# Last three blocks of an attention and FFN kernel: where the normalisation runs, how late squares are added, and the order of the last five steps

## The chip, the core and the metric

The kernel runs on one core of one Trainium2 chip. The metric is the device time in microseconds (us) of one execution. The core has five engines with instruction streams of their own, which meet only through semaphores: TensorE (PE, matmuls; PEld is its weight load), VectorE (DVE), ScalarE (ACT), GpSimd (POOL) and SyncE (SP, which here only issues DMAs). Each engine works its queue in order, so an instruction that waits holds up everything written behind it on the same engine.

## The reference, cut to what matters

The input is 8 sequences of 1024 tokens with 256 channels, in float32. It passes through an attention layer, a layernorm, an FFN and a last layernorm:

```python
x = _layernorm(x + attn(x))          # linear attention, 16 heads, state per sequence
x = _layernorm(x + ffn(x))           # what follows is ffn
h = layer_norm(x, ln1_g, ln1_b)
h = h @ ternary_quant(w1).T + b1     # 256 -> 1024
h = gelu(h)
h = layer_norm(h, ln2_g, ln2_b)      # over the 1024 hidden units
out = h @ ternary_quant(w2).T + b2   # 1024 -> 256
```

The second `layer_norm` needs, for each token, the sum and the sum of squares of 1024 hidden values. The kernel takes the norm out of the product: it multiplies the plain gelu values with w2 and corrects by mean and variance afterwards. The last `_layernorm` is, for each token, `x * rs + sh`, with `rs` the inverse root of the variance and `sh = -mean * rs`. That multiply-add is the "normalisation" of this change.

## The kernel before, in words

The tokens are cut into 16 blocks of 512 (`blocks`, numbered 0 to 15); each block is four tiles of 128 tokens by 256 channels. The program walks through steps; in step i several blocks are in work at once, at different stages: the attention of a block first, then its FFN, then its normalisation. Steps 16 to 20 only drain what is left. What every engine does, and in which order, is written out by hand: the lists in `ORDER` (line 901) hold one word for each piece of work, and `piece` (line 945) issues it. The lists "16" to "20" belong to the last five steps. The words that matter here:

- `H` issues one chunk of the hidden layer (`hidden`, line 653): a block has 8 chunks of 128 hidden units. On TensorE four matmuls (L661) fill one PSUM bank; then ScalarE does the gelu (L667), the upper half of a split of the value into two parts (L670, "u0") and the square (L651). VectorE adds the lower half (L688, "u1", in `lower`; for every third chunk of blocks 13 and 14 it does u0 as well, L687). Below, H14.3 is chunk 3 of block 14, and gelu 14.3, sq 14.3, u0 14.3, u1 14.3 are its steps. u1 is what gives the PSUM bank back. There are two banks named `ph` for H and one named `tp`.
- `A` and `B` issue the second product for one chunk (L733), for tiles 0 and 1 (`A`) and tiles 2 and 3 (`B`), four matmuls each. After chunk 7 ScalarE copies the result out (L746, `z`).
- `ti` transposes the FFN's input of a block (L633); ScalarE writes one part of it (L637, "hThi"), VectorE the other (L638, "hTlo"). All four parts of a block must stand before its first H can end.
- The squares of a block are summed in the tile `sums`: the first two chunks are written there directly, chunks 2 to 5 are added by DMAs that GpSimd issues (L696, two of them), and for blocks 13 and 14 the pair of chunks 6 and 7 is added by one GpSimd instruction over 128x1024 (L694). `sh` then adds the tile's two halves (L712), `sq` transposes the sums on TensorE (L718, "psq") and VectorE reduces them (L720, "sn"). For block 15 GpSimd adds the halves and chunk 6 (two L712), and `sr` adds chunk 7 on VectorE.
- `m` takes steps from queues of small VectorE work (`more`). One such sequence, `rest` (line 794), follows each block's `sq`: statistics of the hidden layer, a power on GpSimd (L143), the two big additions into x per tile (L805, L810), and the statistics of x (`bn_stats` L814, `bn_aggr` L816). Its `rs` is then used in the `rest` of the next block.
- `finish` (line 841) is the normalisation: VectorE makes `sh` (L844), GpSimd does four multiply-adds of 128x256 (L847, "fin"), SyncE sends the block out (L850). It is called for block i-1 in the middle of `rest` of block i, and for block 14 at the end of its own. Block 15 is done apart, by halves (L828 to L839).
- `p` issues one multiply-add of the first layernorm on ScalarE (L894), and `en` four GpSimd instructions that need them (L616).

Three PSUM banks named `w` are handed round: in the last blocks the two B results, the bank of psq and two `ti` take the next one each, and a taker waits until the last user's data are read.

Of the kernel before, what the change touches and what calls it, by code (L numbers as in the profile page):

```python
# [11 lines left out]
AF = mybir.ActivationFunctionType  # L12
ALU = mybir.AluOpType
# [12 lines left out]
def attn_ffn_postln_kernel(  # L26
# [11 lines left out]
    nc = tc.nc  # L38
    B, N, C = x.shape
    HID = w1.shape[1]  # L40
    D = 16
    H = C // D
# [24 lines left out]
    blocks = [(b, g) for b in range(B) for g in range(NB)]  # L67
    xs = {}

    def of_block(dram, i):  # L70
        b, g = blocks[i]
        return dram[b].rearrange("(p t) c -> p t c", p=P)[:, g * G : (g + 1) * G, :]

    def load(i):
        if i < len(blocks):
            xs[i] = xpool.tile([P, G, C], F32, tag="x", name=f"x_{i}")
            nc.sync.dma_start(xs[i], of_block(x, i))
# [247 lines left out]
    def x_of(i):  # L325
        return xs[i]
# [279 lines left out]
    h0, hT, ph, u, sq, sqs, sums, sn, pf, mv, rs, sc, ms, zs = ({} for _ in range(14))  # L606
# [76 lines left out]
    def lower(n):  # L683

        i, j = n // HC, n % HC
        if upper_on_vector(n):
            nc.vector.tensor_scalar(u[n][:, 0, :], ph[n], gm[:, j : j + 1], None, ALU.mult)  # L687
        nc.vector.scalar_tensor_tensor(  # L688
            u[n][:, 1, :], ph[n], gm[:, j : j + 1], u[n][:, 0, :].bitcast(F32),
            ALU.mult, ALU.subtract,  # L690
        )
        if j % 2 == 1 and 1 < j < (HC if i < len(blocks) - 1 else HC - 2):
            if i > len(blocks) - 4 and j == HC - 1:
                nc.gpsimd.tensor_tensor(sums[i], sums[i], sq[i], ALU.add)  # L694
            else:
                nc.gpsimd.dma_start(sums[i], sq[i], accum_op=ALU.add)  # L696

    def upper_on_vector(n):

        return len(blocks) - 4 < n // HC < len(blocks) - 1 and n % 3 == 1  # L700
# [93 lines left out]
    def rest(i, tiles):  # L794
# [3 lines left out]
        if 0 < i < len(blocks) - 1:  # L798
            finish(i - 1, rs[i - 1])
# [24 lines left out]
        if i < len(blocks) - 1:  # L824
            finish(i, r)
            return
# [14 lines left out]
    def finish(i, rs):  # L841

        sh = small.tile([P, G], F32, tag="sh", name=f"sh_{i}")
        nc.vector.scalar_tensor_tensor(sh, mv[i][:, :, 0], -1.0, rs, ALU.mult, ALU.mult)  # L844
        for t in range(G):
            x_t = x_of(i)[:, t, :]
            nc.gpsimd.tensor_scalar(  # L847
                x_t, x_t, rs[:, t : t + 1], sh[:, t : t + 1], ALU.mult, ALU.add
            )
        nc.sync.dma_start(of_block(out, i), x_of(i))  # L850
        load(i + XBUFS)

# [36 lines left out]
    def apply(n):  # L889

        for _ in range(n):
# [19 lines left out]
            m1 m3 ti0/ph B m2 m3 B m m2 p p B sh  # L911
        """,
        "16": """
            p H m1 m2 m6 p H st0/tp m3 A H sq/w m H m st1/tp A H A m8 H A st2/tp st3/w m1 H A m2
            A H tq0/w m1 p m3 a/tp m4 A a/w A a/w m3 tq1/pf a/ph p m2 a/w a/w B B p m4 en m1 m2 p
            m4 a/tp m B sh B B B m m1 ti0/ph m2 m ti1/ph a/tp m p m1
        """,
        "17": """
            m4 m4 B B H m3 m4 m1 H sq/w en m2 B p A m8 H m4 H p A B m4 H m4 ti1/ph en p p m3 A H
            A H A p p p p m4 H A B B A p B  # L920
        """,
        "18": """
            m4 m6 B m3 sh ti0/ph m1 B A B p H H m4 H m2 p p m1 p H ti1/w A ti0/w sq/w m1 m1 m4 H
            H m1 A B m6 B m1 m3 p H B p H p m1 H A B m2 H A B H sh m1 H m4 m4 B H
        """,
        "19": """
            A B p A p A A p B sq/w m4 m4 H A A H m4 m4 B m1 H B m6 A m8 A sh m4 B A B sr B m4 m2
            m3 A B B sq/w B m4 A
        """,
        "20": """  # L930
            m4 m4 B m4 A m4 p
        """,
    }

# [10 lines left out]
    def piece(what, i):  # L945
# [4 lines left out]
        if what == "H":  # L950
            one = turn("H", CHUNKS)
            if one:
                assert count["ti"] >= (one[0] // HC + 1) * KC
                hidden(one[0])
                if low:
                    lower(low.pop())
                low.append(one[0])
        elif low:
            lower(low.pop())
# [150 lines left out]
```

## Time and profile before

| | us |
|---|---|
| median of 3 runs | 666.11 (665.57 to 666.84) |
| the profiled execution | 667.08 |
| its span in the profile | 665.4 |
| PE busy in the span | 605.4 (91%) |
| DVE busy | 511.3 (77%) |
| ACT busy | 498.3 (75%) |
| POOL busy | 338.6 (51%) |
| mean granted TensorE clock | 0.974 |

The span runs from the first to the last profiled instruction; 1.68 us of the profiled execution lie around it. The busy shares are means over a long steady part, in which PE is nearly always at work, and a drain of some 90 us in which it is not: PE is busy for 0.90 to 1.00 of the stretches from 480 to 570 us, and from 570 to 661 us it stands still in places. The change lies in that drain. Times below are us from the start of the span.

### The profile page before, as it was taken

What the parts mean: (1) busy time and instruction counts of PE and PEld (TensorE: products, weight loads), DVE (VectorE), ACT (ScalarE), POOL (GpSimd) and SP (SyncE); (2) the same over time, 40 slices, a digit from 0 to 9 for tenths busy, and PEclk for the clock granted to TensorE, in tenths of its full rate; (3) what the DMA queues carried; (4) which work ended last, traced back from release to release, by engine and by line L of the source; (5) the groups of instructions that cost most, each with busy time, mean ns of one, the idle gap of its engine ahead of it and who ended that gap; (6) DMA issues with size and microseconds to landing.
All of it is one profiled execution on the core that took longest, in us unless ns stands there. A gap on an engine that the chain in (4) does not pass through costs nothing.

```text
span 665.4 us, 9546 instructions
## 1 busy us (share of the span) xinstructions
PE 605.4 (91%) x3200; PEld 478.2 (72%) x3200; DVE 511.3 (77%) x1448; ACT 498.3 (75%) x939; POOL 338.6 (51%) x315
## 2 busy tenths in 40 slices
PE   5799989999999999999999999999999989778850
PEld 3467657878787787868787887878787777566750
DVE  1666776388877797888978887888878888867886
ACT  2554388798897979787887979797979887758720
POOL 1123453545464645646455646456464644765461
PEclk9999999999999999999999999999999999978875
DMA  8522232545365563637463755635354644372321
GB/s 289 208 33 33 32 49 47 96 80 96 48 159 80 115 122 83 129 67 151 80 149 59 159 79 119 120 82 103 61 121 75 125 75 107 56 119 70 89 63 64
DMA packets 33889, 64.73 MB, mean 97 GB/s; under 512 B 3344, under 2 KB 21776, under 8 KB 33840
## 3 DMA queue, kind: packets, MB, share of 16 engines
q0 software_dynamic: 25328, 43.92, 39.8%
q1 hardware_dynamic: 8240, 19.94, 7.9%
q8 instruction: 25, 0.41, 0.3%
q10 hardware_dynamic: 272, 0.26, 0.1%
q14 instruction: 24, 0.20, 0.1%
HBM read 11.95 MB, written 8.39 MB: 31 GB/s over the span
## 4 chain that ended last, share of the span: by engine, by line
PE 64%; DVE 12%; ACT 10%; DMA 4%; issue 4%; POOL 4%; SPq 1%; POOLq 0%; DVEq 0%
PE ph L661 13%; PE pf L733 11%; PE po L546 9%; PE pk L362 8%; PE pa L451 7%; PE pq L408 6%; DVE u L688 3%; ACT sq L651 2%; ACT ph L667 2%; DMA sums<-sums 2%; PE pth L633 2%; PE ptq L341 1%; PE pte L395 1%; PE ptx L341 1%; DVE x L805 1%
## 5 line engine op out<-in xcount | busy, mean ns | idle before, releaser
L733 PE MATMUL pf<-t,u 128*128 128x258 f32 x1024 | 164.0, 300 | 2.3 <-DVE u L688 1.3
L661 PE MATMUL ph<-hT,t 128*128 128x512 f32 x512 | 149.7, 423 | 13.3 <-DVE u L688 10.0
L733 PEld LDWEIGHTS pf<-t,u 128*128 128x128 f32 x1024 | 141.7, 194 | 14.9 <-DVE u L688 4.1
L688 DVE SCALAR_TENSOR_TENSOR u<-ph,gm,u 128x512 fp32r<-128x512 f32 x128 | 95.3, 748 | 51.8 <-ACT sq L651 47.2
L661 PEld LDWEIGHTS ph<-hT,t 128*128 128x128 f32 x512 | 92.0, 192 | 41.0 <-DVE u L688 16.7
L667 ACT ACTIVATE ph<-ph,bh 128x512 f32<-128x512 f32 x128 | 85.1, 665 | 24.1 <-PE ph L661 23.3
L546 PE MATMUL po<-sm,qT 128*128 128x384 f32 x256 | 93.0, 488 | 0.0
L670 ACT ACTIVATE u<-ph,gm 128x512 fp32r<-128x512 f32 x123 | 84.7, 689 | 4.0
L696 POOL DMA_DIRECT2D sums<-sq x45 | 41.5, 923 | 58.3 <-DMA sums<-sq 17.4
L616 POOL TENSOR_SCALAR h<-x,rs_all 128x256 f32<-128x256 f32 x64 | 64.6, 1208 | 7.2 <-ACT x L894 6.2
L651 ACT ACTIVATE sq<-ph,shift 128x512 f32<-128x512 f32 x96 | 65.4, 682 | 0.1
L143 POOL TENSOR_TENSOR ny_y<-nvy,mhalf 128x8 f32<-128x8 f32 x16 | 27.1, 1696 | 74.7 <-DVE nvy L585 74.7
L435 POOL TENSOR_TENSOR q<-q,rq 128x1024 f32<-128x1024 f32 x16 | 31.4, 1962 | 61.2 <-DVE rq L434 59.1
L451 PE MATMUL pa<-x,ek 128*128 128x256 f32 x256 | 60.6, 380 | 0.2 <-ACT ek L399 0.2
L408 PE MATMUL pq<-wqkv_sb,xT 128*128 128x256 f32 x256 | 58.8, 382 | 0.0
L362 PE MATMUL pk<-xT,wqkv_sb 128*128 128x512 f32 x128 | 58.0, 593 | 0.4 <-DVE q L412 0.4
L546 PEld LDWEIGHTS po<-sm,qT 128*128 128x128 f32 x256 | 43.8, 190 | 20.2 <-ACT sm L533 3.0
L422 POOL TENSOR_TENSOR q<-q,qm 128x1024 f32<-128x1024 f32 x16 | 30.9, 1933 | 52.2 <-DVE qm L421 50.1
L451 PEld LDWEIGHTS pa<-x,ek 128*128 128x128 f32 x256 | 47.4, 190 | 9.5 <-ACT ek L399 0.9
L408 PEld LDWEIGHTS pq<-wqkv_sb,xT 128*128 128x128 f32 x256 | 48.5, 191 | 8.0 <-issue 1.2
L637 ACT ACTIVATE hT<-pth,gs 128x512 fp32r<-128x512 f32 x32 | 21.9, 688 | 33.3 <-PE pth L633 33.3
L143 POOL TENSOR_TENSOR ny_f<-nv_f,mhalf 128x8 f32<-128x8 f32 (+2 forms) x17 | 26.6, 1563 | 30.5 <-DVE nv_f L780 30.4
(171 smaller groups left out, 1149.1 us busy)
## 6 DMA issues: line engine op xcount, KB each, us to landing
sums<-sq POOLq DMA_DIRECT2D x45, 512.0 KB, 4.6
x<-in_x_dram SPq DMA_DIRECT2D x16, 512.0 KB, 6.6
x<-crow POOLq DMA_DIRECT2D x16, 512.0 KB, 5.5
x<-bout POOLq DMA_DIRECT2D x16, 512.0 KB, 5.5
out_dram<-x SPq DMA_DIRECT2D x15, 512.0 KB, 2.7
sums<-sums POOLq DMA_DIRECT2D x13, 256.0 KB, 6.1
w<-in_w_dram SPq DMA_DIRECT2D x4, 512.0 KB, 8.0
wqkv_sb<-in_wqkv_dram SPq DMA_DIRECT2D x2, 256.0 KB, 6.7
```

Of the source, the lines that this page charges most:

```text
L143: nc.gpsimd.tensor_tensor(y, v, mhalf[:, :n], ALU.pow)
L362: nc.tensor.matmul(pk, wqkv_sb[:, k, C + c * P : C + (c + 1) * P], xT[i][:, k, :], start=(k == 0), stop=(k == KC - 1),)
L408: nc.tensor.matmul(pq[:, n, :], xT[i][:, k, (t + n) * P : (t + n + 1) * P], wqkv_sb[:, k, 0:C], start=(k == 0), stop=(k == KC - 1),)
L451: nc.tensor.matmul(pa[i][:, c, :], ek[i][:, t, c * P : (c + 1) * P], x_of(i)[:, t, :], start=(t == 0), stop=(t == G - 1),)
L546: nc.tensor.matmul(po[:, c * P : c * P + P + C], qT[i][:, c, t * P : (t + 1) * P], sm[b][:, c, :], start=(c == 0), stop=(c == KC - 1), ski ...
L616: nc.gpsimd.tensor_scalar(h0[i][:, t, :], x_of(i)[:, t, :], rs2[:, t : t + 1], None, ALU.mult)
L651: nc.scalar.activation(sqs[n], ph[n], AF.Square, bias=shift)
L661: nc.tensor.matmul(ph[n], t1[:, k, j * P : (j + 1) * P], hT[i][s][:, k, :], start=(s == 0 and k == 0), stop=(s == 1 and k == KC - 1),)
L667: nc.scalar.activation(ph[n], ph[n], AF.Gelu, bias=bh[:, j : j + 1])
L670: nc.scalar.activation(u[n][:, 0, :], ph[n], AF.Copy, scale=gm[:, j : j + 1])
L688: nc.vector.scalar_tensor_tensor(u[n][:, 1, :], ph[n], gm[:, j : j + 1], u[n][:, 0, :].bitcast(F32), ALU.mult, ALU.subtract,)
L733: nc.tensor.matmul(pf[i, m][t], u[n][:, s, (2 * m + t) * P : (2 * m + t + 1) * P], t2[:, j, :], start=(j == 0 and s == 0), stop=(j == HC - ...
```

## The change

Three things change, all in the last blocks.

1. `finish` for blocks 13 and 14 uses four ScalarE activations (Identity, with bias and scale) in place of four GpSimd `tensor_scalar`. Blocks 0 to 12 keep GpSimd.
2. The addition of chunks 6 and 7 into `sums` for blocks 13 and 14 becomes two GpSimd instructions over 128x512 each.
3. The lists "16" to "20" are replaced.

```diff
             if i > len(blocks) - 4 and j == HC - 1:
-                nc.gpsimd.tensor_tensor(sums[i], sums[i], sq[i], ALU.add)
+                for s in range(2):
+                    half = sums[i][:, s, :]
+                    nc.gpsimd.tensor_tensor(half, half, sq[i][:, s, :], ALU.add)
...
         for t in range(G):
-            x_t = x_of(i)[:, t, :]
-            nc.gpsimd.tensor_scalar(
-                x_t, x_t, rs[:, t : t + 1], sh[:, t : t + 1], ALU.mult, ALU.add
-            )
+            x_t, sh_t, rs_t = x_of(i)[:, t, :], sh[:, t : t + 1], rs[:, t : t + 1]
+            if i < len(blocks) - 3:
+                nc.gpsimd.tensor_scalar(x_t, x_t, rs_t, sh_t, ALU.mult, ALU.add)
+            else:
+                nc.scalar.activation(x_t, x_t, AF.Identity, bias=sh_t, scale=rs_t)
...
         "17": """
-            m4 m4 B B H m3 m4 m1 H sq/w en m2 B p A m8 H m4 H p A B m4 H m4 ti1/ph en p p m3 A H
-            A H A p p p p m4 H A B B A p B
+            p m4 B H m3 m4 m1 H m4 sq/w en m2 m4 B p A m8 H H p B A m4 H m4 ti1/ph en p m3 A H A
+            H A p p p p m4 H A B B A p sh B
         """,
         "18": """
-            m4 m6 B m3 sh ti0/ph m1 B A B p H H m4 H m2 p p m1 p H ti1/w A ti0/w sq/w m1 m1 m4 H
-            H m1 A B m6 B m1 m3 p H B p H p m1 H A B m2 H A B H sh m1 H m4 m4 B H
+            m4 p m6 B m3 ti0/ph m4 m4 B m1 A p B H H H m2 p p m1 p H ti1/w A m1 sq/w m1 m1 m1 m4
+            H H A p m1 B m6 B ti0/w m1 m3 p H H p H m1 A B m2 H A B H m3 H sh B m2 B m1 B H m2 A
         """,
         "19": """
-            A B p A p A A p B sq/w m4 m4 H A A H m4 m4 B m1 H B m6 A m8 A sh m4 B A B sr B m4 m2
-            m3 A B B sq/w B m4 A
+            A A p p A p B sq/w m8 H A m2 A H p B m1 p B m6 m8 A m2 sh H m4 B sr A B B A m2 B m3 B
+            B A sq/ph B A
         """,
         "20": """
-            m4 m4 B m4 A m4 p
+            m4 m4 m4 m3 m2 p A
         """,
```

(List "16" changes in the same way; its words shift by a place or two.) Read out word by word, the new lists give these orders on the engines, beside the old ones:

- TensorE: the second `ti` of block 15 goes from before H14.4 to after B14.1, just ahead of H14.6. psq 13 goes ahead of H14.4 by one place with it. B14.2 to B14.4 go behind one H each, and B14.6 goes from the run of six products behind H15.4 to the place ahead of H15.4. H15.7 goes behind B15.1 and A15.2. At the end B15.7 and A15.5 come ahead of psq 15, and only A15.6 and A15.7 follow it. psq 15 takes a `ph` bank. In the round of the `w` banks psq 14 now follows B14's first bank.
- ScalarE: hThi 15.1 goes from before gelu 14.4 to between sq 14.5 and gelu 14.6. The four fin of block 13 stand between sq 15.6 and gelu 15.7, those of block 14 behind sq 15.7.
- VectorE: hTlo 15.1 goes from before sn 13 to behind the power of block 13. L810 of tile 0 of block 13 goes ahead of u0 and u1 14.6. L805 of tile 2 of block 13 goes ahead of u1 15.1. u1 15.7 goes from between the first L805 and L810 of block 14 to behind the second `bn_stats` of block 14. `sr` goes ahead of the last `bn_aggr` of block 14 and the statistic that starts its last power. The end of that power and the `sh` of block 14 move from before sn 15 to among the statistics of block 15. The `bn_stats` of tile 2 of block 15 moves behind those of tiles 0 and 1.
- GpSimd: for block 13 the two half additions and the L712 now stand in one row ahead of the fin of block 11 (before: L694, fin of block 11, L712). For block 14 the L712 stands behind the DMA for chunks 2 and 3 of block 15 (before: right behind L694). The fin of blocks 13 and 14 are gone.
- SyncE: the outputs leave in the same order.

More of the change, by code (lines that the diff above doesn't have):

```diff
@@ L913, in attn_ffn_postln_kernel @@
         "16": """
-            p H m1 m2 m6 p H st0/tp m3 A H sq/w m H m st1/tp A H A m8 H A st2/tp st3/w m1 H A m2
-            A H tq0/w m1 p m3 a/tp m4 A a/w A a/w m3 tq1/pf a/ph p m2 a/w a/w B B p m4 en m1 m2 p
-            m4 a/tp m B sh B B B m m1 ti0/ph m2 m ti1/ph a/tp m p m1
+            p H m1 m2 m6 p H st0/tp m3 A m1 H sq/w m H A st1/tp m H A m8 H st2/tp st3/w m3 H A A
+            m2 A H m1 tq0/w p m3 a/tp A a/ph m4 A a/w m3 tq1/pf a/ph m2 a/w a/w B B p en m4 m4 m1
+            m2 p m a/tp B sh B B B m m m1 ti0/ph m2 ti1/ph B a/tp m p m1
         """,
         "17": """
-            m4 m4 B B H m3 m4 m1 H sq/w en m2 B p A m8 H m4 H p A B m4 H m4 ti1/ph en p p m3 A H
-            A H A p p p p m4 H A B B A p B
+            p m4 B H m3 m4 m1 H m4 sq/w en m2 m4 B p A m8 H H p B A m4 H m4 ti1/ph en p m3 A H A
+            H A p p p p m4 H A B B A p sh B
         """,
         "18": """
-            m4 m6 B m3 sh ti0/ph m1 B A B p H H m4 H m2 p p m1 p H ti1/w A ti0/w sq/w m1 m1 m4 H
-            H m1 A B m6 B m1 m3 p H B p H p m1 H A B m2 H A B H sh m1 H m4 m4 B H
+            m4 p m6 B m3 ti0/ph m4 m4 B m1 A p B H H H m2 p p m1 p H ti1/w A m1 sq/w m1 m1 m1 m4
+            H H A p m1 B m6 B ti0/w m1 m3 p H H p H m1 A B m2 H A B H m3 H sh B m2 B m1 B H m2 A
         """,
         "19": """
-            A B p A p A A p B sq/w m4 m4 H A A H m4 m4 B m1 H B m6 A m8 A sh m4 B A B sr B m4 m2
-            m3 A B B sq/w B m4 A
+            A A p p A p B sq/w m8 H A m2 A H p B m1 p B m6 m8 A m2 sh H m4 B sr A B B A m2 B m3 B
+            B A sq/ph B A
         """,
         "20": """
-            m4 m4 B m4 A m4 p
+            m4 m4 m4 m3 m2 p A
         """,
```

## The prediction

> **What bounds the drain now.** I read the busy time by stretches first. It shows where the time can come from:
>
> ```profile
> 595.00:600.00 5.00, 2.79 (x15) 2.03 (x14) 4.93 (x8) 2.05 (x6) 2.71 (x2) 1.00 0.22 42
> 600.00:605.00 5.00, 1.95 (x7) 1.27 (x6) 4.83 (x13) 3.99 (x7) 3.50 (x5) 0.87 0.25 105
> ...
> 625.00:630.00 5.00, 5.00 (x30) 4.82 (x30) 4.44 (x15) 2.51 (x7) 0.00 (x0) 0.74 0.55 105
> 630.00:635.00 5.00, 5.00 (x37) 4.65 (x35) 2.46 (x9) 4.79 (x8) 2.54 (x2) 1.00 0.21 43
> 635.00:640.00 5.00, 3.12 (x27) 2.92 (x25) 4.83 (x13) 0.82 (x2) 4.13 (x5) 1.00 0.38 78
> 640.00:645.00 5.00, 0.00 (x0) 0.00 (x0) 4.79 (x12) 0.00 (x0) 2.22 (x3) 0.63 0.22 93
> ```
>
> The columns are the stretch, its length, busy PE, PEld, DVE, ACT and POOL, the granted TensorE clock and the DMAs. From 595 to 605 and from 635 to 645 VectorE is full (4.8 to 4.9 of 5) and TensorE is not (1.95 and 0.00). So a microsecond of VectorE counts there; TensorE's counts in 625 to 630, where it is full at a clock of 0.74.
>
> Next, the timeline says what VectorE does there (start, duration, engine, line, instruction, count; in brackets the idle time before it and who ended it):
>
> ```profile
> 597.29 2.66 POOL L694 TENSOR_TENSOR sums<-sums,sq 128x1024 f32<-128x1024 f32 x1 [4.91 <-DMA sums<-sq]
> ...
> 598.29 1.94 DVE L810 SCALAR_TENSOR_TENSOR x<-g2sum,ms,x 128x256 f32<-128x256 f32 x1
> ...
> 603.85 2.07 PE L661 MATMUL ph<-hT,t 128*128 128x512 f32 x4 [3.05 <-DVE u L688]
> ...
> 618.32 2.40 POOL L694 TENSOR_TENSOR sums<-sums,sq 128x1024 f32<-128x1024 f32 x1 [0.97 <-DMA sums<-sq]
> ...
> 618.80 2.20 DVE L805 SCALAR_TENSOR_TENSOR x<-z,sc,x 128x256 f32<-128x256 f32 x1
> ...
> 620.80 1.34 POOL L712 TENSOR_TENSOR sums<-sums 128x512 f32<-128x512 f32 x1
> 621.04 1.38 DVE L810 SCALAR_TENSOR_TENSOR x<-g2sum,ms,x 128x256 f32<-128x256 f32 x1
> ...
> 623.13 1.20 PE L661 MATMUL ph<-hT,t 128*128 128x512 f32 x4 [1.82 <-DVE u L688]
> 624.17 4.54 PE L733 MATMUL pf<-t,u 128*128 128x258 f32 x24
> ```
>
> L805 and L810 take 0.48 elsewhere. Here they take 1.38 to 2.20, and each ends 0.28 after the GpSimd addition ends: 600.23 after 599.95, 621.00 after 620.72, 622.42 after 622.14. An addition of two SBUF tiles on VectorE is thus held until GpSimd's is done, then let in before GpSimd's next. What reads PSUM (u1 at 602.29 to 605) or one tile (`bn_stats`, 0.43 during L435 at 495.35) is not held. Two of these holds reach TensorE: u1 14.0 comes late, so H14.3 waits 3.05; u1 15.1 comes late, so H15.4 waits 1.82.
>
> **The halves, block 13.** [...] u0 and u1 14.0 are 1.0 earlier, so H14.3 starts at 602.9: -1.0. GpSimd itself does 4.0 us of additions for 3.9 before, and its next work (DMA at 607.64) has 4.1 us of idle time ahead. The fin of block 11, behind them, ends at 604.0 and only an output waits for it.
>
> **hThi and hTlo 15.1, and L810 13.0.** ScalarE has no idle time from 609.31 to 623.76. hThi (0.70) used to lie ahead of that and now lies in it: the 1.0 shrinks to 0.3 at gelu 14.6. On VectorE hTlo (0.73) now stands behind the power of block 13 and L810 (0.48) ahead of u0 and u1 14.6, whose bank H15.1 waits for: sq 14.5 ends at 611.95, then u1 14.5 0.74, power 0.6, hTlo 0.70, three small 0.5, L805 and L810 0.95, u0 and u1 1.45 give 616.85; before, H15.1 started at 616.81. So all of the 1.0 is given back there: 0.0 at gelu 15.1. If nothing had been gained before, the same row would be 0.6 late.
>
> **The halves, block 14.** Its second DMA is issued behind the power of block 13, some 1.5 earlier (611.9 for 613.56), and lands 4.6 later (613.56 to 618.2 before): halves at 616.7 to 619.3. They hold the first L805 13.1 by some 0.8, where L694 and L712 held two by 1.72 + 0.90. L712 is issued only behind the DMA for block 15, which waits for sq 15.3 (623.7): it meets `bn_stats`. u1 15.1 ends at about 621.2 (before 623.08), though one more L805 stands ahead of it. H15.4 then follows B14.4 to B14.6 without a wait, at 622.6, and ScalarE's 0.61 of idle time before gelu 15.4 goes: -0.6.
>
> **B14.6 out of the run.** Behind H15.4 stand 20 matmuls in place of 24, at 0.19 each (4.54 / 24) or at 0.123 (4.91 / 40, at 633.21, clock 1.00). psq 14 now waits for the copy of B14's first bank (two of the four, 0.3 each, about 0.5 behind the last product). At the slow rate H15.5 comes 0.5 earlier, at the fast 1.7. In the trace the slow stretch follows the wait of 1.82, and the rows without such a wait before them (611 to 616, 631 to 638) run fast; the wait goes, so I take -1.7.
> [...]
>
> **ScalarE's new instructions.** A 128x256 Identity takes 0.594 (L894, median of 64; four in a row 2.07). Fin 13 follows its `sh`; behind it wait gelu, u0 and sq 15.7 (0.66 + 0.69 + 0.68): 4.1 us after `sh`. VectorE has eight additions (3.7) and two `bn_stats` (1.1) before it wants u1 15.7, and holds besides, so this costs nothing; without the holds' cover the margin is 0.7. Fin 14 has ScalarE to itself. GpSimd loses 3.13 + 2.18, which brings little: the two L712 of block 15 must wait for a DMA issued at 632.61 (landed 637.2 at 4.6), 1.8 before they used to start, and still hold two additions.
> [...] Here Identity (574.58 to 576.65) stands between Square and Gelu without a gap, so by the trace nothing is added.
>
> **The last chain.** `sr` goes ahead of a `bn_aggr` and a small one: 644.36 comes -0.35. Then psq 15 and sn 15, and VectorE runs the statistics of both halves with the `bn_stats` of tile 2 (0.55) put where VectorE waits for a power: before, the waits were 0.93 and 0.81. The last power of block 14 ends some 0.4 before VectorE wants it. The last normalisations follow as before: -0.2. The order changes of steps 16 and 17 lie before 580, where VectorE and GpSimd wait for the same rows in both; a bank lost or won there is worth at most the 0.4 that PE waits at 546.42, either way: 0.
>
> **Sum**, against the profiled execution (667.08, span 665.4): -1.0 + 1.0 - 0.6 - 1.1 (the rest of -1.7) + 0 - 0.35 - 0.2 = -2.25, span 663.15. That execution is 0.97 above the median, and I take the difference to be the same: 666.11 - 2.2 = 663.9. With a full clock at H14.3 too (2.07 to 1.09) up to 1.0 more goes: 662.9.
>
> **Rivals.**
> - *The slow stretch stays* (the clock falls by itself): -0.5 - 0.35 - 0.2 = -1.05, 665.1. For it: the clock also fell at 641 to 650 in idle time alone. 13%.
> - *The halves are one hold*: GpSimd starts the second before VectorE gets in, and L810 waits until 600.2 as before. Then hThi and hTlo cost their 0.6 at H15.1, and the tail is left: -0.5, 665.6. For it: 0.08 lies between two GpSimd additions (620.72, 620.80). 12%.
> - *Slower: the row of three holds VectorE throughout.* If L810 at 598.4 is not let in until the third addition ends, 597.72 + 3 x 1.34 + 0.28 = 602.0 in place of 600.23, then H14.3 is 1.8 later and nothing is there to take it up, because ScalarE is full from 609 on: -0.45 + 1.8 = +1.4, 667.5. It decides from a hold past 601.9. Against it: in both rows where two additions follow each other one VectorE instruction got in between. 18%.
>
> **Chances.** 57% for the forecast, own range 662.5 to 664.8. 0.2% (1.33 us) is about what a measurement of this kernel tells from no change: faster 57%, within 25% (the first two rivals), slower 18%. The range goes from 662.3 (clock up everywhere, a little more) to 667.0, which leaves out most of the third rival and little below.
>
> **What would show it.** L810 near 598.3 takes under 1.3 and H14.3 waits about 2; no VectorE addition over 1.5 between 616 and 624; H15.4 without a wait; the run behind it at 0.13 a matmul; no gap around the Identities; psq 15 near 642. An L810 over 3 us, or gelu 15.7 behind the wish for u1 15.7, would prove me wrong.

## The result, and the profile after

| us | before | after |
|---|---|---|
| median of 8 runs each, side by side | 667.34 (665.57 to 668.83) | 663.88 (661.26 to 666.66) |
| ratio | | 0.9942, 95% interval 0.9920 to 0.9964 |
| the profiled execution, its span | 667.08, 665.4 | 664.61, 662.9 |
| psq 12 to the last VectorE instruction | 87.73 | 82.67 |
| of it: psq 12 to psq 13 | 34.24 | 30.75 |
| psq 13 to psq 14 | 20.80 | 20.48 |
| psq 14 to `sh` of block 13 | 7.05 | 7.13 |
| `sh` of block 13 to `sr` | 8.76 | 8.08 |
| `sr` to the end | 16.88 | 16.23 |

The changed kernel is faster, by 0.58% (0.36 to 0.80%), or 3.9 us of 667.34. The profiled execution is 2.5 us shorter, but its drain is 5.06 shorter: it comes to psq 12 at 576.11 where the one of before came there at 573.51. Those 2.60 arise ahead of the drain: the granted clock of this execution was 0.99 from 100 to 200 us and 0.98 from 500 to 570, where that of before had 1.00. Over the profiles of all kernels below psq 12 lies between 572.75 and 578.82, and the steady part ahead of it is the same program in all but the words moved in lists 16 and 17 (their worth is measured below). So in what follows the stretches behind psq 12 are compared, besides the times.

The busy time by stretches of the changed kernel, in the columns of the prediction (stretch, length, PE, PEld, DVE, ACT, POOL, granted TensorE clock, DMAs):

```profile
600.00:605.00 5.00, 3.93 (x10) 2.56 (x10) 4.83 (x13) 3.64 (x6) 4.92 (x6) 0.66 0.00 0
...
625.00:630.00 5.00, 4.02 (x30) 3.58 (x29) 4.54 (x17) 3.42 (x9) 2.24 (x3) 1.00 0.57 108
...
635.00:640.00 5.00, 1.89 (x14) 1.49 (x12) 4.86 (x8) 3.54 (x7) 2.70 (x2) 0.85 0.39 131
```

From 625 to 630 the clock is 1.00 where it was 0.74. VectorE is still full at 600 to 605 and at 635 to 640. The low clock has not gone: it lies at 600 to 605 now (0.66 for 0.87).

The timeline of the changed kernel shows the same places as the prediction's (start, duration, engine, line, instruction, count; idle time before it and who ended it). L696 is the addition of chunks 6 and 7 now, L714 the one of the halves, L735 is the second product, L720 is psq, L807 and L812 are the additions into x, L846 is `sh`, L850 the fin on GpSimd and L852 the fin on ScalarE:

```profile
599.74 2.69 POOL L696 TENSOR_TENSOR sums<-sums,sq 128x512 f32<-128x512 f32 x2 [4.93 <-DMA sums<-sq]
...
600.38 0.91 DVE L812 SCALAR_TENSOR_TENSOR x<-g2sum,ms,x 128x256 f32<-128x256 f32 x1
...
600.52 3.83 PE L661 MATMUL ph<-hT,t 128*128 128x512 f32 x9 [2.52 <-DVE hT L638]
604.90 1.20 PE L661 MATMUL ph<-hT,t 128*128 128x512 f32 x4 [0.55 <-DVE u L688]
...
617.61 1.19 PE L661 MATMUL ph<-hT,t 128*128 128x512 f32 x4 [1.51 <-DVE u L688]
...
618.07 2.73 POOL L696 TENSOR_TENSOR sums<-sums,sq 128x512 f32<-128x512 f32 x2 [0.46 <-DMA sums<-sq]
...
618.79 0.85 DVE L807 SCALAR_TENSOR_TENSOR x<-z,sc,x 128x256 f32<-128x256 f32 x1
619.68 1.41 DVE L812 SCALAR_TENSOR_TENSOR x<-g2sum,ms,x 128x256 f32<-128x256 f32 x1
...
622.89 1.09 PE L661 MATMUL ph<-hT,t 128*128 128x512 f32 x4
623.82 2.54 PE L735 MATMUL pf<-t,u 128*128 128x258 f32 x20
625.68 1.60 POOL L714 TENSOR_TENSOR sums<-sums 128x512 f32<-128x512 f32 x1
627.34 0.66 PE L720 MATMUL psq<-ident,sums 128*128 128x128 f32 x4 [0.98 <-POOL sums L714]
...
636.21 1.37 POOL L714 TENSOR_TENSOR sums<-sums 128x512 f32<-128x512 f32 x1 [3.70 <-DMA sums<-sq]
636.38 1.48 DVE L807 SCALAR_TENSOR_TENSOR x<-z,sc,x 128x256 f32<-128x256 f32 x1
...
637.90 1.37 DVE L812 SCALAR_TENSOR_TENSOR x<-g2sum,ms,x 128x256 f32<-128x256 f32 x1
```

The halves do what was expected of them: the held addition of block 12 takes 0.91 (before 1.94), the two held ones of block 13 take 0.85 and 1.41 (2.20 and 1.38), H15.4 has no wait (1.82), and the products behind it run at 2.54 / 20 = 0.127 each (0.19). H14.3 waits 0.55 in place of 3.05, but of these 2.50 only 1.04 are an earlier start, measured from H14.0; in the other 1.46 the matmuls ahead of it run slower (3.83 for 2.37). Two things are new: 1.51 before H15.1 (0.71) and 0.98 of waiting for GpSimd before psq 14. And two additions of block 14 are still held at 636.38 and 637.90, as long as two were before, there those of the next tile (lines of the timeline of before):

```profile
639.19 1.48 DVE L805 SCALAR_TENSOR_TENSOR x<-z,sc,x 128x256 f32<-128x256 f32 x1
640.71 1.37 DVE L810 SCALAR_TENSOR_TENSOR x<-g2sum,ms,x 128x256 f32<-128x256 f32 x1
```

### The profile page after: what moved, and what is told of

It is laid out like the page before. It is cut to its first block, busy times and chain, and to the rows that moved or that the text cites. A ratio compares the mean times of both kernels' runs of the same rounds, so it can differ in the third digit from the quotient of the medians.

```text
span 662.9 us, 9546 instructions
## 1 busy us (share of the span) xinstructions
PE 608.2 (92%) x3200; PEld 479.4 (72%) x3200; DVE 507.2 (77%) x1448; ACT 501.6 (76%) x947; POOL 333.8 (50%) x309
## 4 chain that ended last, share of the span: by engine, by line
PE 70%; DVE 11%; ACT 10%; issue 4%; POOL 3%; DMA 2%; SPq 0%; POOLq 0%; ACTq 0%
PE ph L661 13%; PE pf L735 13%; PE po L546 11%; PE pq L408 7%; PE pk L362 7%; PE pa L451 7%; DVE u L688 2%; ACT ph L667 2%; ACT sq L651 2%; PE pth L633 2%; PE ptq L341 2%; PE ptx L341 2%; PE pte L395 2%; DMA sums<-sums 1%; DMA x<-in_x_dram 1%
## 5 line engine op out<-in xcount | busy, mean ns | idle before, releaser
L735 PE MATMUL pf<-t,u 128*128 128x258 f32 x1024 | 163.3, 299 | 7.2 <-DVE u L688 4.6
L735 PEld LDWEIGHTS pf<-t,u 128*128 128x128 f32 x1024 | 140.6, 192 | 20.3 <-DVE u L688 7.5
L408 PE MATMUL pq<-wqkv_sb,xT 128*128 128x256 f32 x256 | 61.0, 393 | 0.0
L408 PEld LDWEIGHTS pq<-wqkv_sb,xT 128*128 128x128 f32 x256 | 50.0, 197 | 8.7 <-issue 1.2
L362 PEld LDWEIGHTS pk<-xT,wqkv_sb 128*128 128x128 f32 x128 | 24.0, 190 | 24.5 <-issue 20.6
```

Of the source, the lines that this page charges most:

```text
L362: nc.tensor.matmul(pk, wqkv_sb[:, k, C + c * P : C + (c + 1) * P], xT[i][:, k, :], start=(k == 0), stop=(k == KC - 1),)
L408: nc.tensor.matmul(pq[:, n, :], xT[i][:, k, (t + n) * P : (t + n + 1) * P], wqkv_sb[:, k, 0:C], start=(k == 0), stop=(k == KC - 1),)
L735: nc.tensor.matmul(pf[i, m][t], u[n][:, s, (2 * m + t) * P : (2 * m + t + 1) * P], t2[:, j, :], start=(j == 0 and s == 0), stop=(j == HC - ...
```

## The experiments

All in one table: the stretches of the profile as above (us), and the ratio to the kernel before, run on the same chip, side by side. The chips differ a little (medians of before: 667.99, 667.70, 668.06 and 669.93), so ratios are compared, not times.

| kernel | 12 to 13 | 13 to 14 | 14 to `sh` | `sh` to `sr` | `sr` to end | all | ratio (95%) |
|---|---|---|---|---|---|---|---|
| before | 34.24 | 20.80 | 7.05 | 8.76 | 16.88 | 87.73 | 1 |
| scalar_alone | 33.57 | 22.31 | 7.07 | 10.32 | 16.29 | 89.56 | 1.0018 (0.9994 to 1.0042) |
| halves_alone | 31.32 | 17.93 | 7.86 | 8.87 | 16.88 | 82.86 | 0.9965 (0.9941 to 0.9988) |
| halves_scalar | 33.22 | 18.07 | 7.05 | 11.39 | 16.28 | 86.01 | 0.9996 (0.9974 to 1.0018) |
| halves_block13_only | 31.36 | 21.64 | 7.05 | 8.82 | 16.87 | 85.74 | 1.0001 (0.9975 to 1.0026) |
| order_alone | 31.83 | 20.25 | 7.13 | 6.59 | 17.81 | 83.61 | 0.9965 (0.9941 to 0.9989) |
| scalar_order | 33.21 | 20.94 | 7.11 | 8.08 | 16.23 | 85.57 | 0.9971 (0.9947 to 0.9994) |
| halves_order | 30.75 | 20.45 | 7.12 | 6.59 | 17.83 | 82.74 | 0.9969 (0.9940 to 0.9997) |
| after | 30.75 | 20.48 | 7.13 | 8.08 | 16.23 | 82.67 | 0.9942 (0.9920 to 0.9964) |
| late_lists_only | 30.84 | 20.56 | 7.12 | 8.08 | 16.22 | 82.82 | 0.9962 (0.9936 to 0.9987) |
| fin14_on_scalar | 30.76 | 20.34 | 7.11 | 6.59 | 16.15 | 80.95 | 0.9920 (0.9890 to 0.9949) |
| sums_before_dma | 30.74 | 19.79 | 7.05 | 8.08 | 16.21 | 81.87 | 0.9931 (0.9906 to 0.9956) |
| fin14_and_sums | 30.76 | 19.79 | 7.05 | 6.59 | 16.15 | 80.34 | 0.9919 (0.9891 to 0.9947) |
| tail_lists_only | 31.32 | 19.00 | 7.05 | 6.58 | 16.15 | 80.10 | 0.9946 (0.9917 to 0.9974) |

The table tells how far a stretch can be trusted. Up to `sh` of block 13 before and scalar_alone are the same program, and so are halves_alone and halves_scalar: from psq 12 to psq 14 they differ by 0.8 and 2.0. With the new lists and the halves together, six kernels agree within 0.1 from 12 to 13. The two stretches behind `sh` agree within about 0.1 wherever the program there is the same, with one exception: scalar_alone and halves_scalar, 10.32 and 11.39. Each stretch is read from one execution, and the times bear that out only in the main: after, halves_alone, halves_order and late_lists_only have drains of 82.7 to 82.9, and their ratios lie between 0.9942 and 0.9969.

### One part at a time

**halves_alone** takes only the half additions, the lists and the fin as before:

```diff
-                nc.gpsimd.tensor_tensor(sums[i], sums[i], sq[i], ALU.add)
+                for s in range(2):
+                    half = sums[i][:, s, :]
+                    nc.gpsimd.tensor_tensor(half, half, sq[i][:, s, :], ALU.add)
```

> The kernel before with the half additions alone (old lists, normalisation all on GpSimd). Theory (a VectorE addition of two SBUF tiles is held to the end of the GpSimd addition that is running and is then let in): the L810 that took 1.94 near 598 takes about 0.9 to 1.0, H14.3 waits about 2.0 in place of 3.05, and the time falls by 0.5 to 1.3 us (ratio 0.998 to 0.9993). Rival (two additions in a row act as one hold): L810 stays at 1.9, ratio 1.000. Rival (only the order matters): L810 gets shorter but the time stays within 0.3 us.

Its timeline on TensorE, at H14.0, at H14.3 and from H15.4 on:

```profile
600.32 3.92 PE L661 MATMUL ph<-hT,t 128*128 128x512 f32 x9 [2.52 <-DVE hT L638]
605.06 1.21 PE L661 MATMUL ph<-hT,t 128*128 128x512 f32 x4 [0.83 <-DVE u L688]
...
607.82 2.10 PE L661 MATMUL ph<-hT,t 128*128 128x512 f32 x8
...
621.57 1.11 PE L661 MATMUL ph<-hT,t 128*128 128x512 f32 x4
622.52 3.04 PE L735 MATMUL pf<-t,u 128*128 128x258 f32 x24
```

The held addition took 1.27, so GpSimd's two halves are two holds, not one: that rival falls. The gain is larger than the theory's, and H14.3 waits 0.83, not 2.0. TensorE has the same order as before from H14.3 (605.06) to H14.4 (607.82) and needs 2.76 for it, where before needed 4.25 (603.85 to 608.10, with 0.50 of the clock granted from 603.72 to 607.13): 1.5 come from the faster matmuls alone. That part is not sure to come: halves_scalar, the same program to this place, ran slow here (H14.3 took 2.08 for 1.21) and has 33.22 from 12 to 13. At H15.4 there is no wait, and 24 products take 3.04 instead of 4.54 (in before 0.50 of the clock was granted from 624.20 to 627.61): another 1.5 from faster matmuls.

**scalar_alone** takes only the fin of blocks 13 and 14 on ScalarE:

```diff
-            nc.gpsimd.tensor_scalar(...)
+            if i < len(blocks) - 3:
+                nc.gpsimd.tensor_scalar(x_t, x_t, rs_t, sh_t, ALU.mult, ALU.add)
+            else:
+                nc.scalar.activation(x_t, x_t, AF.Identity, bias=sh_t, scale=rs_t)
```

> The kernel before with the normalisation of blocks 13 and 14 on ScalarE alone. Theory (GpSimd is not what the end waits for; its two last additions start with the DMA's landing, about 1.8 us before they used to, and hold two VectorE additions as before): -0.2 to -0.6 us, ratio 0.999 to 0.9997. Rival (taking the normalisation off GpSimd is the main gain): -2 us or more, ratio under 0.997.

Neither theory: no gain in the time (1.0018, the interval holds 1), and by the stretches a loss. `sh` to `sr` is 1.56 longer and `sr` to the end 0.59 shorter. In the old list u1 15.7 stands behind the first L805 of block 14. It needs sq 15.7, which now stands behind four Identities on ScalarE: VectorE waits 3.59 there.

This run shows something else by chance. Its program up to the `sh` of block 13 is that of before, yet the single addition of block 13 caught another VectorE instruction. Its timeline:

```profile
602.45 3.84 PE L661 MATMUL ph<-hT,t 128*128 128x512 f32 x9 [4.29 <-DVE hT L638]
606.59 1.20 PE L661 MATMUL ph<-hT,t 128*128 128x512 f32 x4 [0.30 <-DVE u L688]
```

The L805 ahead of hTlo 14.1 was held for 2.56, and H14.0 waits 4.29 for that part (2.21 in before, where the L810 behind it was caught and H14.3 paid). One addition over 128x1024 thus costs the old order time in either place (12 to 13 is 34.24 and 33.57; with the halves 31.32 to 31.36, or 33.22 where H14.3 ran slow); which place it was differed between these two executions.

**order_alone** takes only the new lists:

```diff
-            m4 m6 B m3 sh ti0/ph m1 B A B p H H m4 H m2 ...
+            m4 p m6 B m3 ti0/ph m4 m4 B m1 A p B H H H m2 ...
...
-            A B p A p A A p B sq/w m4 m4 H A A H m4 m4 ...
+            A A p p A p B sq/w m8 H A m2 A H p B m1 p ...
```

> The kernel before with the five new lists alone: whole additions over 128x1024, normalisation on GpSimd. Theory (the halves give 1.0 us at H14.3 and the order turns it into more): half of the gain of the whole change is left or less, -1 to -2 us, ratio 0.997 to 0.9985; the L810 near 600 is held until the end of the whole addition. Rival (the order does it all): ratio 0.993 to 0.995, as the whole change.

The lists gain as much by themselves as the halves do, 0.9965, a little more than the theory gave them; the L810 near 598 was held to the end of the whole addition as expected (2.16). Half of the gain (2.2 of 4.1 in the drain) is where the prediction saw next to nothing: `sh` to `sr` falls from 8.76 to 6.59. Its timeline there (L847 is the fin on GpSimd, L712 the first of the two additions for block 15, L844 is `sh`, at 632.66):

```profile
632.93 3.52 POOL L847 TENSOR_SCALAR x<-x,ny_f,sh 128x256 f32<-128x256 f32 x4 [2.23 <-DVE sh L844]
...
636.23 0.50 DVE L810 SCALAR_TENSOR_TENSOR x<-g2sum,ms,x 128x256 f32<-128x256 f32 x1
636.43 1.43 POOL L712 TENSOR_TENSOR sums<-sums 128x512 f32<-128x512 f32 x1
...
643.00 2.16 POOL L847 TENSOR_SCALAR x<-x,ny_last,sh 128x256 f32<-128x256 f32 x4 [1.65 <-DVE dev L773]
645.12 0.69 POOL L143 TENSOR_TENSOR ny_f<-nv_f,mhalf 128x2 f32<-128x2 f32 x1
```

With u1 15.7 moved out of VectorE's row, its eight additions are done at 636.7, when GpSimd, busy with the fin until 636.4, has just begun to add: the additions of 1.4 meet `bn_stats`, which is not held: in fin14_on_scalar two of them took 0.41 and 0.39 beside such an addition (L714, 1.42 at 637.22), in before 0.39 to 0.41 with GpSimd idle (642.00 to 644.00). The other side is in the last two lines: the fin of block 14 now stands ahead of the power that the end needs, and VectorE waits 2.28 for that power (`sr` to end: 17.81 for 16.88).

### Two parts at a time

**halves_scalar**, **halves_order** and **scalar_order** join the edits above by twos; the diffs are those shown.

> Both code edits without the new lists. Theory (each edit adds up, and without the lists H15.4 still waits behind u1 15.1 and the run of 24 matmuls stays): -0.8 to -1.8 us, ratio 0.9973 to 0.9988. Rival (the order does it all): ratio 0.999 or above.

> The changed kernel with the normalisation of blocks 13 and 14 back on GpSimd (halves and new lists stay). Theory (ScalarE's four Identities of block 13 free GpSimd too early: its last two additions then meet L807 and L812 of block 14 and cost 1.5 us between the sh of block 13 and sr; behind sr ScalarE gives 0.6 to 1.6 back): sh to sr takes 6.6 in place of 8.1 us, no addition of block 14 is held over 0.7, sr to the end takes 17.5 to 18 in place of 16.2, and the time is that of the changed kernel within 1 us (ratio to before 0.992 to 0.997). Rival (ScalarE's part is worth what the forecast said, GpSimd's load matters): 1.5 us or more slower than the changed kernel, ratio 0.9965 to 0.999.

> The changed kernel with the whole additions over 128x1024 (ScalarE's normalisation and the new lists stay). Theory (the halves give 1.0 at H14.3, most of which is taken back where hTlo 15.1 and L812 stand ahead of u0 14.6): L810 near 598 takes about 2, H14.3 waits over 1.5, and the time is 0.5 to 1.5 us above the changed kernel (ratio 0.9945 to 0.998). Rival (the halves give what they gave alone with the old lists, 2.3 us by the ratio): ratio 0.998 to 1.000.

halves_scalar disappoints as scalar_alone did, for the same reason; its ratio is that of its rival, though the order is not all, as halves_alone shows. On VectorE, in its timeline:

```profile
639.94 0.75 DVE L688 SCALAR_TENSOR_TENSOR u<-ph,gm,u 128x512 fp32r<-128x512 f32 x1 [3.59 <-ACT sq L651]
...
641.00 1.48 DVE L807 SCALAR_TENSOR_TENSOR x<-z,sc,x 128x256 f32<-128x256 f32 x1
```

VectorE stands still for 3.59 in the stretch that bounds the end, and here one addition behind it is held by GpSimd as well (in scalar_alone none is: 10.32 for 11.39). In halves_order and scalar_order the two stretches behind `sh` are 6.59 and 17.83 with the fin on GpSimd and 8.08 and 16.23 with them on ScalarE, so with the new lists these two effects are there with the halves and without. The ratio of halves_order, 0.9969, lies in the range of its theory and in that of its rival; only the stretches tell them apart. scalar_order is in the range for its time but missed both its signs: as in scalar_alone, the L805 ahead of hTlo 14.1 was caught (2.56), H14.0 waits 4.29 and H14.3 only 0.44. The halves and the lists don't add: from psq 12 to psq 14, before and scalar_alone need 55.0 and 55.9, the halves alone 49.3 and 51.3, the lists alone 52.1 and 54.2, and both together 51.2. At H15.4 both take away the same wait: the lists alone leave none. At H14.3 the lists alone bring nothing: it starts 5.64 after H14.0 (5.42 in before), and its wait is down to 1.72 only because the matmuls ahead of it ran slow (3.91 for 2.37).

### What each block's share is

**fin14_on_scalar** is the changed kernel with the fin of block 13 back on GpSimd:

```diff
-            if i < len(blocks) - 3:
+            if i < len(blocks) - 2:
```

> The changed kernel with block 13's normalisation on GpSimd and block 14's on ScalarE. Theory (the two blocks' moves have opposite signs): sh of block 13 to sr 6.6 us without a hold, sr to the end 16.2 us; 1 to 2 us below the changed kernel, ratio to before 0.989 to 0.9935. Rival (both moves gain, or neither counts): not below the changed kernel, ratio 0.994 or above.

Its timeline at the place of the held additions:

```profile
633.72 3.53 POOL L850 TENSOR_SCALAR x<-x,ny_f,sh 128x256 f32<-128x256 f32 x4 [2.21 <-DVE sh L846]
...
637.02 0.50 DVE L812 SCALAR_TENSOR_TENSOR x<-g2sum,ms,x 128x256 f32<-128x256 f32 x1
637.22 1.42 POOL L714 TENSOR_TENSOR sums<-sums 128x512 f32<-128x512 f32 x1
```

No addition takes more than 0.67 in this stretch, and `sr` comes 1.5 sooner after `sh`. The fin of block 13 on GpSimd is of use: it keeps GpSimd's own additions back until VectorE's row is through. The fin of block 14 on ScalarE is worth 1.6 (17.8 to 16.2). This kernel has the lowest median of the study, 662.41. On the same chip late_lists_only, whose drain is that of the changed kernel, has 664.81: the six runs here lie between 659.85 and 663.20, the twelve there between 661.42 and 668.75.

**halves_block13_only** is before with the halves for block 13 alone:

```diff
-                nc.gpsimd.tensor_tensor(sums[i], sums[i], sq[i], ALU.add)
+                for s in range(2 if i == len(blocks) - 3 else 1):
+                    half = sums[i][:, s, :] if i == len(blocks) - 3 else sums[i]
+                    more_sq = sq[i][:, s, :] if i == len(blocks) - 3 else sq[i]
+                    nc.gpsimd.tensor_tensor(half, half, more_sq, ALU.add)
```

> The kernel before with the half additions for block 13 alone; block 14 keeps one addition over 128x1024. Theory (each place has its own gain: at block 13 H14.3 comes earlier, at block 14 the wait of H15.4 and the slow run behind it go): psq 12 to psq 13 falls to 31 to 31.5 us (from 34.2), psq 13 to psq 14 stays at 20 to 21, the wait before H15.4 stays over 1 us; ratio 0.9965 to 0.9995. Rival (the earlier H14.3 alone keeps the clock up and takes the later wait with it): psq 13 to psq 14 falls to about 18 as with both, ratio 0.994 to 0.9965.

The first stretch is that of halves_alone (31.36), the second is not (21.64 for 17.93). Its TensorE there:

```profile
626.39 1.40 PE L661 MATMUL ph<-hT,t 128*128 128x512 f32 x4 [1.96 <-DVE u L688]
627.58 4.40 PE L736 MATMUL pf<-t,u 128*128 128x258 f32 x24
```

With the addition for block 14 in one piece the wait before H15.4 is back, and so is the slow run behind it. The stretches bear the theory out. The drain is 2.0 shorter than that of before, which the time doesn't show: 1.0001 misses the expected range, though its interval of 0.25% to either side reaches into it.

**late_lists_only** is the changed kernel with lists 16 and 17 as before (list 18 begins with the `sh` that 17 now ends with):

```diff
-            H A p p p p m4 H A B B A p sh B
+            A H A p p p p m4 H A B B A p B
...
-            m4 p m6 B m3 ti0/ph ...
+            sh m4 p m6 B m3 ti0/ph ...
```

> The changed kernel with the old lists for steps 16 and 17 (one sh carried to the head of list 18, so that all engines have the changed kernel's order from H14.0 on). Theory (what moves in steps 16 and 17 lies where the same rows end the waits, worth 0 within 0.4 us): the time of the changed kernel within 1 us, ratio 0.992 to 0.997; the stretch from psq 11 to psq 12 the same within 0.5. Rival (the early part of the reordering is where the gain comes from): ratio over 0.997.

82.82 against 82.67, and 32.77 against 32.59 from psq 11 to psq 12. The new lists of steps 16 and 17 do nothing that these runs can tell.

### The new waits

**sums_before_dma** is the changed kernel with the L714 of block 14 ahead of the DMA for chunks 2 and 3 of block 15 on GpSimd's queue:

```diff
-            ... m2 H A B H m3 H sh B m2 B m1 B H m2 A
+            ... m2 H A B H sh m3 H B m2 B m1 B H m2 A
```

> The changed kernel with the addition of block 14's two halves ahead of the DMA for block 15, as it stood before the change (one word of list 18 moved). Theory (in the changed kernel psq 14 waits 0.98 for that addition, because it stands behind a DMA that waits for sq 15.3): the wait of psq 14 for GpSimd goes, the addition holds one more L807 or L812 by up to 1.0 near 621, and psq 13 to psq 14 falls by 0.3 to 1.0 from 20.5. Rival (psq 14 waits for its bank, the copy of B14, or for the run of matmuls): 20.3 to 20.6, no change.

Its timeline on TensorE:

```profile
623.93 2.55 PE L735 MATMUL pf<-t,u 128*128 128x258 f32 x20
626.32 0.60 PE L720 MATMUL psq<-ident,sums 128*128 128x128 f32 x4
```

psq 14 follows the 20 products without a wait, so the 0.98 was GpSimd's queue (the DMA ahead of L714 waits for sq 15.3), not the copy of B14's bank. The stretch falls by 0.7, though L714 now holds one more L807, for 1.51.

**fin14_and_sums** has both edits, that of fin14_on_scalar and that of sums_before_dma.

> The changed kernel with two of its moves taken back: block 13's normalisation on GpSimd again (block 14's stays on ScalarE), and block 14's halves added ahead of the DMA for block 15. Theory (both act in stretches of their own and add up: 1.5 us between the sh of block 13 and sr, 0.7 between psq 13 and psq 14): 80.0 to 80.6 us from psq 12 to the end against 82.7 in the changed kernel and 80.95 with the first alone; ratio to before 0.988 to 0.993. Rival (the earlier psq 14 only moves the wait: GpSimd's normalisation of block 13 then meets VectorE, or the DMA of block 15's squares lands too late for sr): 80.9 or more, no gain over the first alone.

80.34, against 80.95 and 81.87 with one of them: both effects are there. The ratio, 0.9919, is that of fin14_on_scalar.

**tail_lists_only** keeps lists 16 to 18 of before, takes the new order from H15.4 on, the halves, and the fin of block 14 alone on ScalarE:

```diff
-            A A p p A p B sq/w m8 H A m2 A H p B ...
+            A B A A p p A p B sq/w m8 H A m2 A H p B ...
```

> Old lists for steps 16 to 18, the new order from H15.4 on (one A and one B carried over into list 19), half additions for both blocks, block 13's normalisation on GpSimd, block 14's on ScalarE. Theory (the parts of the span add up: 31.3 and 17.9 us between psq 12, 13 and 14 as with the halves alone, 7.1 to 7.9 to the sh of block 13, 6.6 to sr, 16.2 to the end): 79 to 80 us from psq 12 to the end against 82.7 in the changed kernel; 2.5 to 3.5 us below the changed kernel, ratio to before 0.987 to 0.992. Rival (what is gained at H15.4 is lost in the tail, which waits for the DMA of block 15's squares): not below the run with block 14 alone on ScalarE, 0.992 or above.

It has the shortest drain, 80.10, near what was expected (psq 13 to psq 14 is 19.00, not 17.9). H15.4 waits 0.89 here and the run behind it is still fast (24 in 3.03). The ratio, 0.9946, misses what was expected. Its profiled execution came to psq 12 late, at 578.53 (only halves_block13_only came later, at 578.82), in the part that it shares with before, but whether that holds for its other runs can't be told from their times.

fin14_on_scalar, sums_before_dma, fin14_and_sums and tail_lists_only all beat before. None of them can be told from the changed kernel by its time: the intervals of 0.9919, 0.9920, 0.9931, 0.9946 and 0.9942 overlap. That fin14_on_scalar and fin14_and_sums are 1.7 and 2.3 better is a statement on their drains.

## Why the prediction was right, and where it was not

The predicted 663.9 and the measured 663.88 agree better than the reasons do. Measured from hTlo 14.1, where both kernels first wait in the same way (H14.0 starts at 598.43 and at 600.52, so 2.09 later), the steps came out so:

| step | forecast | profile of after |
|---|---|---|
| H14.3 | -1.0 | 603.85 to 604.90: -1.04 |
| gelu 15.1, by H15.1 | 0.0 in all | 616.81 to 617.61: -1.29 in all |
| H15.4 | -0.6 more | 623.13 to 622.89: -1.04 more |
| psq 14 | -1.1 more | 628.55 to 627.34: -0.97 more |
| `sh` of block 13 | 0 | +0.08 |
| `sr` | -0.35 | -0.68 |
| the end | -0.2 | -0.65 |
| sum | -2.25 | -4.55 |

**The direction and the mechanism** were right. In the changed kernel the held addition of block 12 ended at 601.29, behind the first half (599.74 to 601.00) and ahead of the end of the second (600.98 to 602.43), so the halves shortened the hold. This is what halves_alone shows without the rest (1.27 in place of 1.94). The first -1.0 of the sum was the author's estimate; no run shows the term, since no trace of before tells where within the 2.66 of L694 a first half would have ended. What the runs show in its place is that addition at 0.91 for 1.94, and H14.3 1.04 sooner.

**The mis-sized term is the 1.0 at H14.3, "all of the 1.0 is given back there: 0.0 at gelu 15.1".** H14.3 came sooner by the forecast amount. But the matmuls behind it ran at the full clock (1.00 granted from 604.41 to 638.50, where before had 0.50 from 603.72 to 607.13; H14.3 1.20 for 2.07, A14.0 0.72 for 1.04), and the second `ti` of block 15 (0.44) no longer stands there, so that gelu 14.4 came at 608.43 for 609.31, 2.97 earlier by the same measure. The forecast knew of H14.3's part and put it outside the sum ("up to 1.0 more goes"); the `ti` it left out. The order then gave 1.7 back up to H15.1, where 1.0 was forecast: that `ti` at 610.87 (0.35), 0.46 for hTlo 15.1 at 614.66, and 1.51 for u1 14.6 where 0.71 was waited before. That clock is not the halves' doing alone: in scalar_alone, the same program to this place as before, the slow rate lay on H14.0 to H14.2 (3.84 for 2.37) and H14.3 ran fast (1.20), but the wait for hTlo 14.1 was longer instead. So a price read from one execution of such a stretch is uncertain: 12 to 13 is 34.24 and 33.57 in one pair with the same program there, and 31.32 and 33.22 in the other. The sign "H14.3 waits about 2" failed for this reason too.

**H15.4 and the run behind it** came as forecast: no wait, 0.127 a matmul, at a granted clock of 1.00. The rival in which the slow stretch stays falls. In all three kernels with the run of 24 where H15.4 waited 0.89 or less (0.00, 0.62, 0.89), it took 3.03 or 3.04; in the three where it waited 1.82 to 1.96 (before, scalar_alone, halves_block13_only), 3.99 to 4.54. The -1.7 for H15.4 and psq 14 measured -2.01. One reason inside it was wrong: psq 14 waits for GpSimd's queue and not for the copy of a bank.

**"This costs nothing", of the fin of block 13 on ScalarE,** was wrong by 1.5 us. The prediction had both held additions in view, but compared them with the old order, in which two were held as well, for another reason (at 639.19 and 640.71, because u1 15.7 stood ahead of them). With the new lists and the fin on GpSimd nothing is held (6.59 against 8.08). The error stayed hidden because the new lists' gain of 2.2 in that stretch was not forecast either: the two make the 0.68 measured.

**The last chain** gained 0.65 for 0.2: 1.6 from the fin of block 14 on ScalarE, less 0.9 that the lists lose without it. The prediction had GpSimd's relief as "brings little". The Identities themselves came as it said: four in 2.08 at 634.66, and gelu 15.7 behind them at 636.65 without a gap.

**The other rivals.** One hold: it falls, since the held additions of block 12 took 0.83 to 1.46 in all ten kernels with halves there. Three holds, and slower: it falls too, since L812 was done at 601.29, 0.91 after its start, and the third addition began only at 602.50 (the 597.72 that this rival counts from is the end of the L805 at 597.24 in before). One reading was off without a consequence: the 0.4 at 546.42 is the idle time of the weight load, and the matmuls' is 0.20; the term was put at 0 either way.

**Why the time came out right nevertheless:** the drain's 4.55, and 0.5 between psq 12 and H14.0, met 2.60 of a later start of the drain in the profiled execution, and in the medians 3.5 remain (3.9 by the ratio), 1.3 more than the 2.2 forecast from before's 666.11; the kernel before measured 667.34 over eight runs, 1.23 above the median that the forecast started from. So the hit is partly luck: the gain was under-forecast by about as much as the starting point was low. The steady part of one execution takes up to 6 us more than that of another, and this goes with the granted clock: from 0 to 200 us it was 1.00 in the three that came to psq 12 first (before, order_alone and halves_order, 572.75 to 573.51) and 0.97 to 0.98 in the three that came last (halves_scalar, tail_lists_only and halves_block13_only, 577.46 to 578.82). Why it differs was not tested.

## What to carry to other kernels

Where GpSimd and VectorE both add SBUF tiles, look first at what VectorE has in its row when GpSimd starts: here splitting the GpSimd instruction shortened the hold (one VectorE addition took 0.91 for 1.94), and beside statistics, or beside work that reads PSUM, there was none (`bn_stats` 0.41 and 0.39 beside L714 in fin14_on_scalar; u1 0.74 beside L696 at 618.13 in the changed kernel, 0.75 in the mean of before). A piece of work on an engine with time to spare may be what keeps that engine's next piece from coming too early, so "it frees GpSimd" is no gain until the trace shows what GpSimd does with the time. Price a slow-clock stretch by how much of it falls on work that something waits for, and do not take one execution's place of it for the next one's. Where several edits remove the same wait, measure them singly and together: here the halves gave 0.35%, the lists 0.35%, both together 0.31%, and with the third edit, which alone gains nothing, 0.58%, each to about 0.25%.

## What was not expected of the hardware

- Some waits of 1.5 to 3 us were followed by half the clock, and others were not. In before the granted clock is 0.50 from 603.72 to 607.13 (H14.3, at 603.85, had waited 3.05) and from 624.20 to 627.61 (H15.4, at 623.13, had waited 1.82), and 1.00 from 590.25 to 603.72, where H14.0 had waited 2.21, and from 607.13 to 624.20. In the changed kernel it is 0.50 from 601.00 to 604.41 (H14.0, at 600.52, had waited 2.52) and 1.00 from there to 638.50, where H15.1 had waited 1.51. Three rows of before (columns as above; the first number behind the comma is busy TensorE):

```profile
596.89:600.31 3.42, 1.88 (x8) 1.56 (x9) 3.42 (x5) 1.30 (x3) 3.02 (x2) 1.00 0.00 0
600.31:603.72 3.41, 0.49 (x3) 0.05 (x1) 3.24 (x11) 3.34 (x7) 3.19 (x5) 1.00 0.18 73
603.72:607.13 3.41, 3.28 (x11) 2.79 (x12) 1.39 (x3) 1.48 (x3) 0.00 (x0) 0.50 0.21 85
```

- So the wait ahead of H14.0 was followed by slow matmuls in one run and not in another. In before it was 2.21, and H14.0 to H14.2 took 2.37; H14.3, behind the 3.05, took 2.07. In the ten runs whose timelines show 2.51 or more there (scalar_alone and scalar_order 4.29, the changed kernel, halves_alone, halves_block13_only and the five from late_lists_only to tail_lists_only in the table 2.51 to 2.53), H14.0 to H14.2 took 3.73 to 3.93, ahead of H14.3's wait, where this is mostly covered, and H14.3 took 1.19 to 1.21. halves_scalar, the same program to there as halves_alone, waited 2.27, and took 2.96 and, for H14.3, 2.08. What decides where the clock falls was not shown.
- The runs of one kernel spread by 0.8% (661.26 to 666.66 for the changed one), and go, in the main, with the mean granted clock: its fastest run had 0.981, its slowest 0.966. Differences of 0.2 to 0.3% between these kernels need the stretches of the profile beside the times.
- Four GpSimd fin beside VectorE's additions, both on SBUF, lengthened none of them beyond 0.67 (0.48 alone; fin14_on_scalar, at 634.04), while the fin themselves took 3.52 for 2.16 (order_alone); beside an addition of 128x512 on GpSimd one VectorE addition took up to 1.51 (sums_before_dma, at 620.67).
